# Two attention layers and two feed-forward layers on one core: the place of score products, the order of a second burst, and where constants are made

## The chip, the cores and the metric

The kernel runs on one core of a Trainium2 chip. The metric is the device time of one execution, in microseconds. TensorE (PE) multiplies matrices, VectorE (DVE) and ScalarE (ACT) read its results from PSUM, GpSimd (POOL) works from SBUF only, and SyncE (SP) issues the DMAs. PSUM has eight banks here: seven are handed out in rotation (`BANKS = 7`), one belongs to the weighted values.

## What is computed

The input has 4 batches of 2048 tokens with 256 features, in float32. Four sublayers follow each other, each on the layer-normalized input and each added to it:

```python
x = x + _L0_attn_ref(_layernorm(x), ...)   # one causal head, keys and values of 64
x = x + _L0_ffn_ref(_layernorm(x), ...)    # clipped to 8-bit floats, one matrix, a bias
x = x + _L1_attn_ref(_layernorm(x), ...)   # 16 causal heads of 16, rotary positions
x = x + _L1_ffn_ref(_layernorm(x), ...)    # mix with the token before; sigmoid(r) * (relu(k)**2 @ W_v)
```

## The kernel before

**Tiles.** The tokens are cut into 16 blocks of 512, four per batch (`order` lists them as b, qb). A block attends to itself and to the blocks before it in its batch. In the second attention the 16 heads form four groups of four (`HG = 4`); each of a group's heads sits in 32 partitions, so that a product of one head uses one of four row groups of the PE array, and the four heads' products can run beside each other.

**Steps.** The main loop goes over blocks, groups (index G) and tiles of 128 keys (`kt`); a block with index qb has 4, 8, 12 or 16 steps per group, 640 steps in all. In a step each head gets *scores* (`scores_of`): one bank, three products (L809), namely ones times the shift `sh` (the negated maximum of each query, in three bfloat16 parts), and the keys times the high and the low part of the queries. On the diagonal, that is in the last four steps of a group, fewer columns remain (512, 384, 256, 128) and two mask products (L817) follow. ScalarE then makes the exponential p (L824). The *weighted values* (`weighted`, L860) multiply p with the values in column groups of the array.

**Maxima.** Scores need the maximum of each query ahead of them. `maxima_of` makes them for the group that follows: one bank per head, two products (L779), on the diagonal two masks (L788), and a reduction on VectorE (L794). `all_maxima` gives each set its due place, mostly one set of four heads per step.

**The order in a step.** Instructions of PE, ACT, DVE and POOL are issued in the order in which the program writes them. A step writes, in this order: a *first burst* with scores of heads 0 and 1 and maxima of heads 2 and 3; the products that turn a finished group to tokens, if there is one; the weighted values of the step *before*; a *second burst* with maxima of heads 0 and 1 and scores of heads 2 and 3; further maxima if more than one set is due; the shift of the next group at a group's end (`shift_of`); and pulled work, products of other stages for this or other blocks that use the whole array.

```python
together([[S[0]], [S[1]], M[2], M[3]], {h: S[h] for h in (2, 3) if kt})
weighted(*last)
together([M[0], M[1], [S[2]], [S[3]]])
pull(lists, 0.0)
```

`together` writes a burst in rounds, one product per head and round, and passes over a head that has not begun while `room(h)` finds no bank. Its `spare` heads are those whose score may begin in a row that has ended.

**The planner.** `Clock` keeps a book of estimated times while the program is written: when each engine, row group and bank comes free. `room(h)` counts the banks that this book shows as free 50 ns after the last product. `pull` takes generators of other stages (A: first attention and first feed-forward of blocks ahead; Bq and Q: projections, keys and queries of the second attention; E: what follows it) when the book shows their inputs ready and the step's credit lasts; `pull_first` takes the earliest; `force` empties a list.

**The head.** Constants (identities, causal masks, zeroed pads, `ones`, `mask_k`, `mask_q`) are made on POOL ahead of all else, and six DMAs on SP copy the last two to the other row groups. A loop then brings the first block through `a_in` (layer norm, transposition, queries, keys, values; in two halves `hf` of 256 tokens), `a_mid` (first attention), `a_out`, `b_in`, `b_project` (rotation on POOL), `b_keys` and `b_queries`, with the second block's list A2 behind it. In `a_in` the second half waits at its start until the first half's projections are written. `prepare` (seven VectorE operations on weights) is written when its first weight is due in the book within 1 us of PE's time, or when nothing else can be taken.

Of the kernel before, what the change touches and what calls it, by code (L numbers as in the profile page):

```python
# [13 lines left out]
F16 = mybir.dt.float16  # L14
F32R = mybir.dt.float32r
BF16 = mybir.dt.bfloat16
# [3 lines left out]
ALU = mybir.AluOpType  # L20
AX = mybir.AxisListType

P = 128
# [3 lines left out]
TT = BLK // P  # L27
# [3 lines left out]
HG = 4  # L31
NG = NH // HG
SLOT = 32
LN_EPS = 1e-5
NEG = -1e30
# [155 lines left out]
def seq_kernel(  # L191
# [21 lines left out]
    nc = tc.nc  # L213
# [4 lines left out]
    const = ctx.enter_context(tc.tile_pool(name="const", bufs=1))  # L218
    clock = Clock(nc)
# [6 lines left out]

    ident = const.tile([P, P], F32, name="ident")
    make_identity(nc, ident)
    ident_b = const.tile([P, P], BF16, name="ident_b")
    make_identity(nc, ident_b)  # L230
    ident_h = const.tile([P, P], F16, name="ident_h")
    make_identity(nc, ident_h)

    mask_b = const.tile([P, P], BF16, name="mask_b")
    make_causal_mask(nc, mask_b, mask_val=NEG)

    maskT_b = const.tile([P, P], BF16, name="maskT_b")
    nc.gpsimd.memset(maskT_b, 0.0)
    nc.gpsimd.affine_select(
        out=maskT_b, in_=maskT_b, pattern=[[1, P]], compare_op=ALU.is_ge,  # L240
        fill=NEG, base=0, channel_multiplier=-1,
    )
    mhalf = const.tile([P, TT], F32, name="mhalf")
    nc.gpsimd.memset(mhalf, -0.5)

# [17 lines left out]
    order = [(b, qb) for b in range(B) for qb in range(NB)]  # L263
# [54 lines left out]

    pads = []
    for i in range(3):
        t = const.tile([P, TT, HG, SLOT], BF16, name=f"pad{i}")
        nc.gpsimd.memset(t, 0.0)
        pads.append(t)
    ones = const.tile([P, P], BF16, name="ones")
    nc.gpsimd.memset(ones, 0.0)
    for h in range(HG):
        nc.gpsimd.memset(ones[h * SLOT : h * SLOT + 3, :], 1.0)

# [1 line left out]

    mask_k = const.tile([P, 2, P], BF16, name="mask_k")
    mask_q = const.tile([P, 2, P], BF16, name="mask_q")
    for t, first, picks in (
        (mask_k, 0.0, ((ALU.not_equal, 2.0**-22, 0), (ALU.not_equal, 2.0**62, 1))),
        (mask_q, -(2.0**62), ((ALU.is_ge, 0.0, 0), (ALU.not_equal, -(2.0**-22), 0))),  # L340
    ):
        nc.gpsimd.memset(t[:SLOT], first)
        for keep, fill, base in picks:
            nc.gpsimd.affine_select(
                out=t[:SLOT], in_=t[:SLOT], pattern=[[P // 2, 2], [-1, P]],
                compare_op=keep, fill=fill, base=base, channel_multiplier=2,
            )
        for h in range(1, HG):
            nc.sync.dma_start(t[h * SLOT : (h + 1) * SLOT], t[:SLOT])

# [4 lines left out]
    live = [0]  # L355
# [21 lines left out]
    def done(n):  # L377
        live[0] -= n
# [83 lines left out]
    def a_in(b, qb, x, hf):  # L462

        tag = f"a0_{b}_{qb}"
        while hf and (b, qb, "a", 0) not in flags:
            yield None
        to = []
        yield from normal_T(x, to, hf, tag)
        xT = to[0]
        t2 = slice(2 * hf, 2 * hf + 2)  # L470
        nc.gpsimd.tensor_tensor(
            x[:, t2, :], x[:, t2, :], bo_bc[:, None, :].to_broadcast([P, 2, C]), ALU.add
        )
# [12 lines left out]
        nc.scalar.activation(th[:, cols], pq, AF.Identity, bias=bqk)  # L486
        nc.vector.scalar_tensor_tensor(
            tl[:, cols], pq, bqk, th[:, cols].bitcast(F32), ALU.add, ALU.subtract
        )
        if hf:  # L490

            for dst, src in (
                (qh[:D0], th[:D0]), (qh[D0:], th[:D0]), (kT[:D0], th[D0:]),
                (ql[:D0], tl[:D0]), (ql[D0:], tl[:D0]), (kT[D0:], tl[D0:]),
            ):
                nc.sync.dma_start(dst.bitcast(F32), src.bitcast(F32))
# [12 lines left out]
        flags.add((b, qb, "in", hf))  # L509
# [287 lines left out]
    def scores_of(b, qb, g, kt, sh, pTs, h):  # L797

        r = slice(h * SLOT, (h + 1) * SLOT)
        c0 = max(kt - qb * TT, 0) * P  # L800
        keys = kT1[b, kt // TT][r, g, (kt % TT) * P : (kt % TT + 1) * P]
        diag = kt >= qb * TT
        sc = bank(f"s_{b}_{qb}_{g}_{kt}_{h}")

        q = q1[b, qb, g // 2]
        todo = [(keys, z[r, g % 2, c0:]) for z in q]
        todo.insert(0 if kt else 2, (ones[r, :], sh[r, c0:]))
        for i, (lhsT, rhs) in enumerate(todo):
            nc.tensor.matmul(  # L809
                sc[:, c0:], lhsT, rhs, start=(i == 0), stop=(i == 2 and not diag)  # L810
            )
# [12 lines left out]
        nc.scalar.activation(pTs[h][:, c0:], sc[:, c0:], AF.Exp, scale=DK**-0.5)  # L824
        yield

    def room(h):

        clock.follow()
        now = max(clock.issue, clock.rows[h]) + 50  # L830
        return sum(b not in clock.held and t <= now for b, t in clock.banks.items())

    def together(rows, spare=()):

        rows = [[[part, False] for part in r] for r in rows]
        spare = dict(spare)
        wait = True
        while any(rows):  # L840
            moved = False
            for h, r in enumerate(rows):
                while r:
                    if wait and not r[0][1] and not room(h):
                        break
                    try:
                        next(r[0][0])
                        r[0][1] = moved = True
                        wait = True
                        break  # L850
                    except StopIteration:
                        r.pop(0)
                if not r and h in spare and any(rows) and room(h) > 3:
                    next(spare.pop(h))
            wait = moved

# [284 lines left out]
    a_next = 2  # L1141
    live[0] += 3
    prepared = False
    while Bq or Q or len(A2) > 2:
        credit = 1.0
        if not pull([Bq, Q, A], 0.0):
            credit = 0.1
            if not pull([A2], 0.0):
                ripe = not prepared and clock.when(wfs[0]) < clock.pe + 1000
                if ripe or not pull_first([Bq, Q, A, A2]):  # L1150
                    assert not prepared, (live, [(g.__name__, asked.get(id(g))) for l in (Bq, Q, A, A2) for g in l])
                    prepare()
                    done(3)
                    clock.follow()
                    prepared = True
        while narrow:
            narrow_values()
    A.extend(A2)
# [31 lines left out]
    for G, (i, b, qb, g) in enumerate(groups):  # L1190
# [5 lines left out]
        for kt in range(n):  # L1196
# [19 lines left out]
            if last is not None:  # L1216
# [4 lines left out]
                if last[2] != g:  # L1221
# [105 lines left out]
```

## Time and profile before

| | us |
|---|---|
| median of 3 runs | 2928.36 (2923.62, 2928.36, 2931.43) |
| the profiled execution | 2922.84 |
| its span, first to last instruction | 2921.0 |
| L809, three score products per head, busy | 672.6 + 494.3 + 481.0 |
| L779, two maxima products per head, busy | 686.1 + 559.3 |
| L860, weighted values, busy | 641.0 |
| L824, exponentials on ACT, busy; mean of one | 1214.2; 0.534 |
| L794, reductions on DVE, busy; mean of one | 1405.1; 0.603 |

The span is what lies between the first and the last instruction on the chip; the execution's own time is 1.8 us longer. Busy times of PE overlap, since up to four row groups work at once: the L809 and L779 rows can't be added up to the span, and a busy PE may have empty row groups. Steps of the main loop run from 115.3 us (first score product) to 2883.7 us (start of the last weighted group).

### The profile page before, as it was taken

The numbers are of one execution on the slowest core, as the hardware profiler recorded it, in microseconds if no ns is written. First come the engines' busy times: TensorE is split into PE (matmuls) and PEld (weight loads), VectorE is DVE, ScalarE is ACT, GpSimd is POOL, SyncE is SP. The second block draws the span as 40 slices with busy tenths as digits, with TensorE's granted clock in tenths as the row PEclk, the third lists the DMA queues.
The fourth block names the chain that finished last, engine by engine and source line by source line (L and its number), as shares of the span: only waits on it lengthen the run. The fifth ranks groups of instructions, "written<-read, shape, count | busy, mean of one in ns | idle before, by whom it ended". The sixth has DMA issues, their size and how long they took to land.

```text
span 2921.0 us, 68258 instructions
## 1 busy us (share of the span) xinstructions
PE 2804.3 (96%) x27616; PEld 1580.6 (54%) x27616; DVE 2012.6 (69%) x4279; ACT 1688.2 (58%) x3553; POOL 1011.8 (35%) x1534
## 2 busy tenths in 40 slices
PE   6899999999999999999999999999999999999997
PEld 3555555555456555555556555555545655555443
DVE  4567667787556786787746777778764677678761
ACT  2456555566665556656665555656566565665663
POOL 4534425242333514514215342523323342450001
PEclk8799999999999999999999999999999999999999
DMA  3000000000000000000000000000000000000000
GB/s 91 1 12 5 12 12 16 12 2 26 2 12 16 5 23 2 16 12 5 23 12 5 12 5 23 5 23 1 27 2 12 16 5 16 1 9 1 5 1 12
DMA packets 28781, 36.70 MB, mean 13 GB/s; under 512 B 3312, under 2 KB 22064, under 8 KB 28464
## 3 DMA queue, kind: packets, MB, share of 16 engines
q1 hardware_dynamic: 28464, 32.32, 3.9%
q8 instruction: 217, 3.56, 0.5%
q14 instruction: 100, 0.82, 0.1%
HBM read 11.24 MB, written 8.39 MB: 7 GB/s over the span
## 4 chain that ended last, share of the span: by engine, by line
PE 79%; DVE 11%; POOL 5%; issue 3%; ACT 1%; DMA 0%; SPq 0%; POOLq 0%; ACTq 0%; DVEq 0%
PE av L860 18%; PE s L809 16%; PE m L779 14%; DVE mx L794 7%; PE pq_a L421 3%; PE pv_a L421 2%; PE av_a L578 2%; PE m_a L524 2%; PE po_f L421 2%; PE pk_f L928 2%; PE pw_f L421 2%; PE pr_f L421 2%; PE m L788 1%; PE s_a L548 1%; PE pt_c L871 1%
## 5 line engine op out<-in xcount | busy, mean ns | idle before, releaser
L794 DVE TENSOR_REDUCE mx<-m 128x1 f32<-128x512 f32 (+3 forms) x2560 | 1405.1, 603 | 531.6 <-PE m L779 237.6
L824 ACT ACTIVATE p<-s 128x512 f32<-128x512 f32 (+3 forms) x2560 | 1214.2, 534 | 814.3 <-PE s L809 445.8
L779 PE MATMUL m<-kT_a,qh_a 32*128 32x512 f32 (+3 forms) x2560 | 686.1, 458 | 13.7 <-ACT p L824 4.0
L809 PE MATMUL s<-qh_a,kT_a 32*128 32x512 f32 (+3 forms) x2560 | 672.6, 508 | 0.5 <-ACT p L824 0.5
L860 PE MATMUL av<-p,v_a 128*32 128x512 f32 (+3 forms) x5120 | 641.0, 545 | 0.1
L779 PEld LDWEIGHTS m<-kT_a,qh_a 32*128 32x128 f32 x2560 | 296.0, 184 | 493.9 <-issue 161.1
L779 PE MATMUL m<-kT_a,ql_a 32*128 32x512 f32 (+3 forms) x2560 | 559.3, 368 | 0.0
L809 PE MATMUL s<-ql_a,kT_a 32*128 32x512 f32 (+3 forms) x2560 | 494.3, 365 | 0.0
L809 PE MATMUL s<-sh,ones 32*128 32x512 bf16 (+3 forms) x2560 | 481.0, 355 | 3.1 <-DVE mx L794 2.3
L779 PEld LDWEIGHTS m<-kT_a,ql_a 32*128 32x128 f32 x2560 | 297.0, 188 | 3.3 <-issue 1.0
L809 PEld LDWEIGHTS s<-qh_a,kT_a 32*128 32x128 f32 x2560 | 259.7, 189 | 35.3 <-issue 23.7
L809 PEld LDWEIGHTS s<-ql_a,kT_a 32*128 32x128 f32 x2560 | 257.3, 187 | 2.8 <-issue 0.2
L809 PEld LDWEIGHTS <-ones 32*128 32x128 bf16 x2560 | 128.7, 91 | 171.4 <-issue 150.5
L860 PEld LDWEIGHTS av<-p,v_a 128*32 128x32 f32 x5120 | 112.4, 108 | 161.8 <-issue 118.7
L443 POOL CAST pad<-nm 128x16 bf16<-128x16 f32 x64 | 17.0, 266 | 380.9 <-DVE nm L989 352.3
L590 POOL TENSOR_TENSOR sum_a<-sum_a,p_a 128x512 f32<-128x512 f32 (+1 forms) x128 | 146.3, 1143 | 5.0
L788 PE MATMUL m<-mask_k,mask_q 32*128 32x64 bf16 x2048 | 147.0, 196 | 0.0
L817 PE MATMUL s<-mask_q,mask_k 32*128 32x64 bf16 (+1 forms) x2048 | 140.4, 207 | 0.0
L590 POOL TENSOR_TENSOR cx_a<-cx_a,avs_a 128x512 f32<-128x512 f32 (+1 forms) x64 | 73.1, 1143 | 155.1 <-ACT avs_a L588 155.1
L421 PE MATMUL pq_a<-wqkv,xT_a 128*128 128x512 f32 x256 | 122.8, 602 | 1.6 <-DVE mx L794 1.3
L950 POOL TENSOR_TENSOR x<-x,sg_f 128x512 f32<-128x512 f32 x32 | 41.4, 1294 | 177.3 <-DVE sg_f L949 177.1
L935 POOL TENSOR_TENSOR ka_f<-ka_f 128x512 f32<-128x512 f32 x32 | 33.2, 1038 | 186.1 <-ACT ka_f L934 186.1
(164 smaller groups left out, 4015.6 us busy)
## 6 DMA issues: line engine op xcount, KB each, us to landing
x<-in_x SPq DMA_DIRECT2D x16, 512.0 KB, 4.0
out_y<-x SPq DMA_DIRECT2D x32, 256.0 KB, 2.1
qh_a<-th_a SPq DMA_DIRECT2D x32, 128.0 KB, 2.3
ql_a<-tl_a SPq DMA_DIRECT2D x32, 128.0 KB, 2.3
kT_a<-th_a SPq DMA_DIRECT2D x16, 128.0 KB, 2.3
kT_a<-tl_a SPq DMA_DIRECT2D x16, 128.0 KB, 2.3
wqkv<-in_wqkv1T SPq DMA_DIRECT2D x1, 768.0 KB, 7.3
wc<-in_wfT SPq DMA_DIRECT2D x1, 256.0 KB, 5.7
```

Of the source, the lines that this page charges most:

```text
L421: nc.tensor.matmul(dst, lhsT[:, k, t * P : (t + 1) * P], w[:, k, :], start=(k == 0), stop=(k == CK - 1),)
L524: nc.tensor.matmul(sc[:, :w], q[:, t * P : (t + 1) * P], kT0[kb][:, :w], start=(q is qh), stop=(kb < qb and q is ql),)
L578: nc.tensor.matmul(av[z * SLOT : (z + 1) * SLOT, c0:], v0[kt // TT][:, kt % TT + j, d * SLOT : (d + 1) * SLOT], pTs[j][:, c0:], start=True ...
L590: nc.gpsimd.tensor_tensor(to[:, c0:], to[:, c0:], add[:, c0:], ALU.add)
L779: nc.tensor.matmul(sc[:, :w], q1[b, qb, g // 2][i][r, g % 2, t * P : (t + 1) * P], kT1[b, kb][r, g, :w], start=(i == 0), stop=(kb < qb and ...
L788: nc.tensor.matmul(sc[:, w - P + lo : w - P // 2 + lo], mask_q[r, v, :], mask_k[r, v, lo : lo + P // 2], start=False, stop=(v == 1),)
L794: nc.vector.reduce_max(mx[:, t, h, kb : kb + 1], sc[:, :w], axis=AX.X)
L809: nc.tensor.matmul(sc[:, c0:], lhsT, rhs, start=(i == 0), stop=(i == 2 and not diag))
L817: nc.tensor.matmul(sc[:, c0 : c0 + hi], mask_k[r, v, :], mask_q[r, v, :hi], start=False, stop=(v == 1),)
L824: nc.scalar.activation(pTs[h][:, c0:], sc[:, c0:], AF.Exp, scale=DK**-0.5)
L860: nc.tensor.matmul(av[h * SLOT : (h + 1) * SLOT, c0:], v1[b, kt // TT][:, kt % TT, at : at + SLOT], pTs[h][:, c0:], start=(kt == 0), stop= ...
L928: nc.tensor.matmul(pk[:, d * HALF : (d + 1) * HALF], wk[:, k, d * P : (d + 1) * P], xk[:, k, :], start=(k == 0), stop=(k == CK - 1),)
```

## The change

Three parts, in one diff.

1. *First bursts.* A spare score (head 2 or 3) begins if `room(h)` is over 0 instead of over 3. A head that begins so is noted in `early`, and its products then stand in the order keys times high queries, ones times shift, keys times low queries, so that what is written in the first burst is a product with the keys. In the second burst the remaining two follow.
2. *Second bursts.* Heads are gone through in the order 2, 3, 0, 1: scores of 2 and 3 ahead of maxima of 0 and 1.
3. *The head of the run.* All constants but the float32 identity, `mhalf` and `one` move into `constants()`, written once the first block's first half has begun its projections, with the six DMAs. In the first block the second half's layer norm and transposition no longer wait for the first half's projections; its own projections still do. `prepare` is written once the second half's values are projected. The line with 1000000000.0 is never true, so the second block's list is asked as before when nothing else is ready.

```diff
-    ident_b = const.tile([P, P], BF16, name="ident_b")
-    make_identity(nc, ident_b)
...
-        for h in range(1, HG):
-            nc.sync.dma_start(t[h * SLOT : (h + 1) * SLOT], t[:SLOT])
+
+    def constants():
+
+        make_identity(nc, ident_b)
+
+        make_causal_mask(nc, mask_b, mask_val=NEG)
+
+        nc.gpsimd.memset(maskT_b, 0.0)
...
+        for t in reversed(pads):
+            nc.gpsimd.memset(t, 0.0)
...
+        make_identity(nc, ident_h)
...
+            for h in range(1, HG):
+                nc.sync.dma_start(t[h * SLOT : (h + 1) * SLOT], t[:SLOT])
...
-        while hf and (b, qb, "a", 0) not in flags:
+        while hf and (b, qb) != order[0] and (b, qb, "a", 0) not in flags:
             yield None
         to = []
         yield from normal_T(x, to, hf, tag)
         xT = to[0]
+        while hf and (b, qb, "a", 0) not in flags:
+            yield None
...
-        todo.insert(0 if kt else 2, (ones[r, :], sh[r, c0:]))
+        todo.insert((1 if h in early else 0) if kt else 2, (ones[r, :], sh[r, c0:]))
...
+    early = set()
+
...
-    def together(rows, spare=()):
+    def together(rows, spare=(), order=range(HG)):
...
-            for h, r in enumerate(rows):
+            for h in order:
+                r = rows[h]
...
-                if not r and h in spare and any(rows) and room(h) > 3:
+                if not r and h in spare and any(rows) and room(h) > 0:
+                    early.add(h)
                     next(spare.pop(h))
...
+    made = False
     while Bq or Q or len(A2) > 2:
+        if not made and (*order[0], "a", 0) in flags:
+            constants()
+            clock.follow()
+            made = True
+        if not prepared and (*order[0], "in", 1) in flags:
+            prepare()
+            done(3)
+            clock.follow()
+            prepared = True
...
-            if not pull([A2], 0.0):
-                ripe = not prepared and clock.when(wfs[0]) < clock.pe + 1000
-                if ripe or not pull_first([Bq, Q, A, A2]):
...
+            ahead = [clock.free[e] for e in ("act", "dve", "pool")]
+            if (ready and max(ahead) > ready + 1000000000.0) or not pull([A2], 0.0):
+                some = pull_first([Bq, Q, A, A2])
...
+            early.clear()
             together([[S[0]], [S[1]], M[2], M[3]], {h: S[h] for h in (2, 3) if kt})
...
-            together([M[0], M[1], [S[2]], [S[3]]])
+            together([M[0], M[1], [S[2]], [S[3]]], order=(2, 3, 0, 1))
```

More of the change, by code (lines that the diff above doesn't have):

```diff
@@ L228, in seq_kernel @@
     make_identity(nc, ident)
-    ident_b = const.tile([P, P], BF16, name="ident_b")
-    make_identity(nc, ident_b)
[L231 to L242, printed above, removed]
     mhalf = const.tile([P, TT], F32, name="mhalf")
@@ L313, in prepare @@
         nc.vector.tensor_scalar_mul(wv_flat, wv_flat, 0.5)
[L321 to L325, printed above, removed]
+    ident_b = const.tile([P, P], BF16, name="ident_b")
+    ident_h = const.tile([P, P], F16, name="ident_h")
+    mask_b = const.tile([P, P], BF16, name="mask_b")
+    maskT_b = const.tile([P, P], BF16, name="maskT_b")
+    pads = [const.tile([P, TT, HG, SLOT], BF16, name=f"pad{i}") for i in range(3)]
@@ L326, in seq_kernel @@
     ones = const.tile([P, P], BF16, name="ones")
-    nc.gpsimd.memset(ones, 0.0)
-    for h in range(HG):
-        nc.gpsimd.memset(ones[h * SLOT : h * SLOT + 3, :], 1.0)
     mask_k = const.tile([P, 2, P], BF16, name="mask_k")
     mask_q = const.tile([P, 2, P], BF16, name="mask_q")
[L338 to L347, printed above, removed]
-        for h in range(1, HG):
-            nc.sync.dma_start(t[h * SLOT : (h + 1) * SLOT], t[:SLOT])
+    def constants():
+        make_identity(nc, ident_b)
+        make_causal_mask(nc, mask_b, mask_val=NEG)
+        nc.gpsimd.memset(maskT_b, 0.0)
+        nc.gpsimd.affine_select(
+            out=maskT_b, in_=maskT_b, pattern=[[1, P]], compare_op=ALU.is_ge,
+            fill=NEG, base=0, channel_multiplier=-1,
+        )
+        for t in reversed(pads):
+            nc.gpsimd.memset(t, 0.0)
+        nc.gpsimd.memset(ones, 0.0)
+        for h in range(HG):
+            nc.gpsimd.memset(ones[h * SLOT : h * SLOT + 3, :], 1.0)
+        make_identity(nc, ident_h)
+        for t, first, picks in (
+            (mask_k, 0.0, ((ALU.not_equal, 2.0**-22, 0), (ALU.not_equal, 2.0**62, 1))),
+            (mask_q, -(2.0**62), ((ALU.is_ge, 0.0, 0), (ALU.not_equal, -(2.0**-22), 0))),
+        ):
+            nc.gpsimd.memset(t[:SLOT], first)
+            for keep, fill, base in picks:
+                nc.gpsimd.affine_select(
+                    out=t[:SLOT], in_=t[:SLOT], pattern=[[P // 2, 2], [-1, P]],
+                    compare_op=keep, fill=fill, base=base, channel_multiplier=2,
+                )
+            for h in range(1, HG):
+                nc.sync.dma_start(t[h * SLOT : (h + 1) * SLOT], t[:SLOT])
@@ L1147, in seq_kernel @@
             credit = 0.1
-            if not pull([A2], 0.0):
-                ripe = not prepared and clock.when(wfs[0]) < clock.pe + 1000
-                if ripe or not pull_first([Bq, Q, A, A2]):
[L1151 to L1155, printed above, removed]
+            ready = [start_of(gens, gen) for gens in (Bq, Q, A) for gen in list(gens)]
+            ready = min([t for t in ready if t is not None] or [0.0])
+            ahead = [clock.free[e] for e in ("act", "dve", "pool")]
+            if (ready and max(ahead) > ready + 1000000000.0) or not pull([A2], 0.0):
+                some = pull_first([Bq, Q, A, A2])
+                if not some:
+                    assert some, (live, [(g.__name__, asked.get(id(g))) for l in (Bq, Q, A, A2) for g in l])
         while narrow:
```

## The prediction

> **What bounds the kernel now.** I read the page first, then busy time by stage, then the order of time inside a few steps of the main loop, and last the head of the run.
>
> ```profile
> span 2921.0 us, 68258 instructions
> PE 2804.3 (96%) x27616; PEld 1580.6 (54%) x27616; DVE 2012.6 (69%) x4279; ACT 1688.2 (58%) x3553; POOL 1011.8 (35%) x1534
> PE 79%; DVE 11%; POOL 5%; issue 3%; ACT 1%; DMA 0%; SPq 0%; POOLq 0%; ACTq 0%; DVEq 0%
> ```
>
> TensorE is busy for 96% of the span and 79% of the chain that ended last lies on it. By stage:
>
> ```profile
> 0.00:33.00 33.00, 13.54 (x54) 11.02 (x54) 14.10 (x37) 4.46 (x7) 15.44 (x42) 0.86 0.56 177
> 33.00:115.00 82.00, 62.28 (x348) 41.24 (x348) 37.15 (x105) 23.85 (x48) 52.18 (x74) 0.81 0.05 10
> 115.00:2866.00 2751.00, 2688.42 (x26970) 1505.65 (x26968) 1950.16 (x4111) 1643.73 (x3463) 934.86 (x1405) 0.99 0.04 11
> ```
>
> (Columns: length, then busy time of PE, weight loads, DVE, ACT, POOL, granted clock, DMA share and rate.) From 115 us to 2866 us PE is busy for 2688 of 2751 us at a clock of 0.99: only less PE time per step helps there. The head is another regime: 76 of 115 us busy. So the question is what a step costs on PE, and a "busy" product may use only two of the four row groups. Two steps in order of time:
>
> ```profile
> 1505.22 0.39 PE L809 MATMUL s<-sh,ones 32*128 32x512 bf16 x2
> 1505.26 0.58 PE L809 MATMUL s<-qh_a,kT_a 32*128 32x512 f32 x2
> 1505.68 0.40 PE L809 MATMUL s<-ql_a,kT_a 32*128 32x512 f32 x2
> 1506.01 0.65 PE L415 MATMUL pt_a<-ident,xn_a 128*128 128x128 f32 x4
> 1506.60 0.39 PE L809 MATMUL s<-sh,ones 32*128 32x512 bf16 x2
> 1506.64 0.58 PE L809 MATMUL s<-qh_a,kT_a 32*128 32x512 f32 x2
> 1507.06 0.40 PE L809 MATMUL s<-ql_a,kT_a 32*128 32x512 f32 x2
> 1507.39 1.07 PE L860 MATMUL av<-p,v_a 128*32 128x512 f32 x8
> 1508.39 0.39 PE L809 MATMUL s<-sh,ones 32*128 32x512 bf16 x2
> ```
>
> At 1505.22 a second burst: heads 2 and 3, three products each, 0.79 us to the next work. At 1506.01 a pulled transpose on the whole array. At 1506.60 the first burst of the next step: heads 0 and 1, three products, while rows 2 and 3 stand empty. Then the weighted values, and at 1508.39 heads 2 and 3 once more. In the burst at 1506.60 there is room for the first product of heads 2 and 3. One product of 512 columns takes 0.23 us: (1505.68 - 1505.22) / 2, from the start of the first to the start of the third.
>
> **First-burst products, the main part.** In the old code the spare rows start a score only with more than three banks free. Counting score products (L809) up to each weighted group shows that this happened 19 times in 640 steps. Now one free bank does, in the 576 steps with kt above 0. Per step one product moves from the second burst to rows that are idle in the first (maxima have two products, scores three). Nothing is added: the same 7680 score products.
>
> Where does it pay? Bursts that follow each other with nothing between run rows independently: rows 0 and 1 do two maxima and three score products, rows 2 and 3 three and two, five each, and moving one from a burst to the burst before changes no sum. It pays where whole-array work is pulled between second burst and next first burst, since there the array drains and the time is 3 + 3 products against 2 + 3. Such work stands behind 424 of the 576 steps; 257 of them have full width (512 columns). The other 167 are on the diagonal (384, 256, 128 columns): there maxima of two long products already outlast three short score products, so the moved product lengthens the first burst about as much as it shortens the second. Summing row lengths over those steps gives a gain of 0 to 3 us; I take 0.
>
> Both rows must be granted a bank, for with one row still at three products the second burst is as long as before. I paired each PSUM tile's first product with the instruction that empties it, and counted banks outside such pairs 50 ns after the second head's third product began. Of the 257 full, pulled steps 197 had one free or more and 120 two or more. As a test of this count: more than three were free in 13 steps, against 19 that the old rule granted. So 120 x 0.23 = 28 us as it stands; 257 x 0.23 = 59 us if every grant came; about 1 us if the kernel's own book of bank times has one bank fewer free than the trace. Counted 0.4 us later, at that product's end, 169 steps have two free (39 us). I take 140 steps, nearer to the first count: 32 us.
>
> A check of "idle rows cost nothing": 166 second bursts with maxima beside the scores (four rows) took 0.88 us from first start to last end, the one at 1508.39 with two rows 0.85 us. Two more rows cost 0.02 us over three products, so nothing is charged. The Trainium skill, page "TensorE: Matmul & The Clock Gate", section "Measured speedup vs the span model", has a rule against it: four row tiles give 3.07 times, not four times. By that a filled slot would cost 0.3 of a product and the 32 us would become an estimated 22. The two bursts above differ by far less, and they decide.
>
> **Order of the second burst.** Scores of heads 2 and 3 go ahead of maxima of heads 0 and 1. The maxima's bank wait no longer stands before the scores; behind the scores stand only the maxima, then their reductions on VectorE, needed a group later. In the trace the second burst starts 0.52 us after the last weighted product in the median of 303 full-width cases (mean 0.525), which is the mode change, so few banks are missing there and the order alone gains or loses little: bounds plus and minus 3 us, value 0.
>
> **The exponentials' chain.** Weighted products wait for p of heads 2 and 3 in few steps: 51 groups are over 0.1 us longer than their width asks for, 37 us in all, 48 of them without pulled work behind the burst. There the earlier scores start ACT earlier by one product: 32 of them had a free bank; each gains one product or what its wait lasts, whichever is less: 6 us together. Bounds 0 and 10.
>
> **Constants, first half, prepare.** 22 POOL instructions (1.31 to 8.42 us without mhalf and one) and six DMAs on SP leave the head.
>
> ```profile
> 8.42 0.22 POOL L395 TENSOR_SCALAR v_a<-mv_a 128x2 f32<-128x2 f32 x1
> 8.72 0.72 POOL L397 TENSOR_TENSOR y_a<-v_a,mhalf 128x2 f32<-128x2 f32 x1
> 14.34 1.85 SPq L349 DMA_DIRECT2D mask_k<-mask_k  x3
> 16.29 1.80 SPq L349 DMA_DIRECT2D mask_q<-mask_q  x3
> 20.23 0.71 POOL L397 TENSOR_TENSOR y_a<-v_a,mhalf 128x2 f32<-128x2 f32 x1
> 29.09 0.60 SPq L496 DMA_DIRECT2D kT_a<-tl_a  x1
> 32.74 0.46 PE L524 MATMUL m_a<-kT_a,qh_a 128*128 128x128 f32 x1
> ```
>
> The first y (the scale of the layer norm, made on POOL) starts at 8.72 because the constants stand ahead; its statistics are done at 6.08, so it comes 2.3 us earlier. The second half's y of the first block stood at 20.23, because the half was only begun behind the first projections, with the 4.3 us of the seven VectorE operations of the old early preparation between (13.36 to 18.18). Now its statistics follow the first half's at once: y near 8. So the queries and keys, whose last copy was issued at 29.09 and was landed for the first product at 32.74, could be ready some 15 us earlier but for what is late next. The constants, 6.9 us on POOL, now begin behind the first x + bo (about 9.5) and end near 16.4; the mask DMAs (1.85 + 1.80 us of SP) wait for them, to about 20; the six copies of q and k (3.7 us) may stand behind those on SP, to 24, and landing takes 2.3 us by the page: 26 or so against 32. Six us at that point. Preparation now runs behind the second half's projections, while PE waits for the copies; if that cover is gone, 4.3 us of VectorE stand before the first maxima's reductions. Masks, ones and pads are first read at 33 us and later, which hides POOL's part; but y and x + bo of the second block are queued behind the constants on POOL, up to 6.9 us late, and from 63 to 80 us POOL is full with that block's sums, for which the first block's rotation (80 to 99) waits. So not all six arrive at 115 us, where the steps begin. Value 5 us, bounds -7 (the constants' length given back by the second block) and +12.
>
> **Sum.** 32 + 0 + 0 + 6 + 5 = 43 us. The profiled execution took 2922.84 us (span 2921.0 and 1.8 around it), so 2880; it was the fastest of four, 5.5 us below the median of 2928.36, and I forecast a median: 2885 us. Its own range: main part 1 to 59, taken as 15 to 50 for the likely cases, others as above: 2865 to 2910.
>
> **Rivals.**
> (a) *Banks take the place.* Early scores hold two of seven banks through the weighted products (1.0 us), and transposes to tokens, narrow values and the maxima of the second burst look for one. For it: no bank was free in 183 of 576 decisions, and maxima of the first burst already stand still for a bank of VectorE in 80 cases, 28.5 us, 0.36 each. If the second burst's maxima wait as long behind 250 early steps, 90 us are lost against 43 won: 2975; it decides from 120 such waits on. Against it: a bank is only taken if one is free, two would be taken at the burst's start anyway, and no stall stands there now. The Trainium skill, "Trainium Kernel Development and Optimization", Best Practices, warns that tiling speeds up TensorE but not the emptying of PSUM; no row here gives that a price beyond the waits counted. Chance 0.15.
> (b) *The grants do not come, or the room is used up*: the book of bank times refuses as before, or pulled work that is now early waits for its inputs instead (VectorE is 71% busy in the main stage, 1950 of 2751). Then 0 to 10 us are left, from the head and the exponentials: 2923. Chance 0.15.
> (c) *All grants come*: 59 + 10 + 10 = 79 us: 2849. For it: less waiting frees banks earlier. Against: ACT and VectorE free banks at their own pace while the next decision comes earlier too. Chance 0.15.
> Forecast: 0.55.
>
> **How the numbers follow.** 2885 is the forecast's. Of (a) nearly all lies above 2937, of (c) half below 2849; the range 2848 to 2936 leaves 0.07 below and 0.13 above. What a measurement can tell from no change is about 0.3%, 9 us: 2919.6 to 2937.1. Faster: 0.53 of the forecast, all of (c), 0.04 of (b), together 0.72. Same: 0.02 of the forecast, 0.07 of (b), 0.01 of (a): 0.10. Slower: 0.14 of (a), 0.04 of (b): 0.18.
>
> **What would show it.** Right: many second bursts with four instead of six score products; in pulled steps 0.56 us instead of 0.79 from burst to next work; score products with qh standing ahead of ones in first bursts; PE's busy time in the main stage down by about what the span loses; the first full-array maxima (L524 now) near 26 us. Wrong: bursts of six as before (b); weight loads of maxima idle behind VectorE in second bursts (a); no shorter burst although the grants came, which would mean that the four rows do not run side by side; the first steps beginning later than 115 us, which would put the head's sign wrong.

## The result, and the profile after

The changed kernel takes 2967.75 us in the median of 4 runs (2966.5 to 2976.93), the kernel before 2928.52 beside it: ratio 1.0142, interval 1.0118 to 1.0167. It is slower by 39 us; 2885 was forecast.

The page of the changed kernel: span, engines' busy time, chain by engine.

```profile
span 2966.7 us, 68223 instructions
PE 2843.0 (96%) x27616; PEld 1613.6 (54%) x27616; DVE 2027.5 (68%) x4279; ACT 1690.7 (57%) x3553; POOL 1013.6 (34%) x1534
PE 79%; DVE 10%; POOL 5%; issue 3%; ACT 2%; DMA 0%; POOLq 0%; ACTq 0%; DVEq 0%
```

The same 27616 products make PE busy 39 us longer; no other engine gained as much. By stage (columns as before; the steps of the main loop begin at 129 us now, 115 before):

```profile
33.00:129.00 96.00, 70.52 (x356) 45.91 (x356) 39.01 (x105) 24.68 (x49) 52.67 (x73) 0.73 0.04 9
129.00:2929.00 2800.00, 2736.27 (x27122) 1540.26 (x27120) 1963.03 (x4111) 1655.37 (x3486) 935.07 (x1404) 0.98 0.04 11
```

So the head is 14 us longer, and the steps are longer as well: from the first weighted group to the last 2794.4 us against 2762.2. I gave the time from each product's start to the next one's to the kind of the earlier one. Bursts went from 1226.1 to 1256.7 us, weighted products from 587.3 to 582.8, pulled work from 948.8 to 954.9. The loss stands in the bursts, where the gain was forecast. Not all of it is what the products of a burst cost: the clock granted to TensorE fell to 0.5 for 121.3 us of the changed kernel's steps and for 66.2 us of the steps before. What that is worth comes at the end of the experiments.

The grants came: counted as before, 252 steps started both spare scores and 283 one. A first burst of the kernel before, with pulled work ahead of it, in order of time:

```profile
434.90 0.39 PE L809 MATMUL s<-sh,ones 32*128 32x512 bf16 x2
434.90 0.50 PE L779 MATMUL m<-kT_a,qh_a 32*128 32x512 f32 x2
434.94 0.58 PE L809 MATMUL s<-qh_a,kT_a 32*128 32x512 f32 x2
435.24 0.40 PE L779 MATMUL m<-kT_a,ql_a 32*128 32x512 f32 x2
435.36 0.40 PE L809 MATMUL s<-ql_a,kT_a 32*128 32x512 f32 x2
435.69 0.64 PE L860 MATMUL av<-p,v_a 128*32 128x512 f32 x4
```

The same kind of burst of the changed kernel, with both spare scores, and a second burst relieved of them:

```profile
1044.07 0.39 PE L811 MATMUL s<-sh,ones 32*128 32x512 bf16 x2
1044.08 0.50 PE L781 MATMUL m<-kT_a,qh_a 32*128 32x512 f32 x2
1044.11 0.58 PE L811 MATMUL s<-qh_a,kT_a 32*128 32x512 f32 x2
1044.41 0.40 PE L781 MATMUL m<-kT_a,ql_a 32*128 32x512 f32 x2
1044.53 0.39 PE L811 MATMUL s<-ql_a,kT_a 32*128 32x512 f32 x2
1044.64 0.40 PE L811 MATMUL s<-qh_a,kT_a 32*128 32x512 f32 x2
1044.97 0.64 PE L866 MATMUL av<-p,v_a 128*32 128x512 f32 x4
...
735.40 0.39 PE L811 MATMUL s<-sh,ones 32*128 32x512 bf16 x2
735.41 0.49 PE L781 MATMUL m<-kT_a,qh_a 32*128 32x512 f32 x2
735.44 0.58 PE L811 MATMUL s<-ql_a,kT_a 32*128 32x512 f32 x2
735.74 0.40 PE L781 MATMUL m<-kT_a,ql_a 32*128 32x512 f32 x2
736.07 0.40 PE L453 MATMUL pt_sh_a<-ident_b,pad 128*128 128x128 bf16 x4
```

Read the starts within one row group. A row that opens with ones (bfloat16) starts its third product 0.46 us after its first (434.90 to 435.36). A row that opens with keys or queries (float32) starts its *second* 0.33 us after the first (1044.08 to 1044.41), and its third at 0.56 (1044.64). So the maxima's row with a third product ends 0.1 us after the score rows beside it: the first burst lasts 0.90 us to the weighted group, instead of 0.79. And the second burst, 0.67 us, goes by the maxima's rows, which open with float32, so it saves 0.13 us and not 0.23.

### The profile page after: what moved, and what is told of

Same layout as the page of the kernel before. It is cut to its first block, busy times and chain, and to the rows that moved or that the text cites. A ratio compares the mean times of both kernels' runs of the same rounds, so it can differ in the third digit from the quotient of the medians.

```text
span 2966.7 us, 68223 instructions
## 1 busy us (share of the span) xinstructions
PE 2843.0 (96%) x27616; PEld 1613.6 (54%) x27616; DVE 2027.5 (68%) x4279; ACT 1690.7 (57%) x3553; POOL 1013.6 (34%) x1534
## 4 chain that ended last, share of the span: by engine, by line
PE 79%; DVE 10%; POOL 5%; issue 3%; ACT 2%; DMA 0%; POOLq 0%; ACTq 0%; DVEq 0%
PE s L811 20%; PE av L866 18%; PE m L781 10%; DVE mx L796 6%; PE pq_a L421 3%; PE pv_a L421 2%; PE av_a L580 2%; PE pk_f L934 2%; PE po_f L421 2%; PE m_a L526 2%; PE pr_f L421 2%; PE pw_f L421 2%; ACT p L826 1%; PE pt_c L877 1%; PE pq_a L486 1%
## 5 line engine op out<-in xcount | busy, mean ns | idle before, releaser
L811 PE MATMUL s<-qh_a,kT_a 32*128 32x512 f32 (+3 forms) x2560 | 733.1, 481 | 4.9 <-ACT p L826 3.4
L781 PE MATMUL m<-kT_a,qh_a 32*128 32x512 f32 (+3 forms) x2560 | 704.9, 462 | 15.7 <-ACT p L826 10.2
L811 PE MATMUL s<-ql_a,kT_a 32*128 32x512 f32 (+3 forms) x2560 | 629.1, 413 | 0.0
L781 PE MATMUL m<-kT_a,ql_a 32*128 32x512 f32 (+3 forms) x2560 | 574.8, 370 | 0.0
L811 PE MATMUL s<-sh,ones 32*128 32x512 bf16 (+3 forms) x2560 | 469.2, 357 | 6.1 <-DVE mx L796 4.9
L781 PEld LDWEIGHTS m<-kT_a,qh_a 32*128 32x128 f32 x2560 | 307.1, 185 | 77.0 <-ACT p L826 36.1
L811 PEld LDWEIGHTS s<-qh_a,kT_a 32*128 32x128 f32 x2560 | 303.5, 188 | 66.4 <-ACT p L826 21.6
L811 PEld LDWEIGHTS s<-ql_a,kT_a 32*128 32x128 f32 x2560 | 305.0, 190 | 2.3
L819 PE MATMUL s<-mask_q,mask_k 32*128 32x128 bf16 (+1 forms) x2048 | 157.1, 208 | 0.0
L532 DVE TENSOR_REDUCE mx_a<-m_a 128x1 f32<-128x512 f32 (+3 forms) x160 | 87.5, 602 | 18.4 <-PE m_a L526 16.2
```

Source lines behind the costliest of these rows:

```text
L532: nc.vector.reduce_max(mx[:, t, kb : kb + 1], sc[:, :w], axis=AX.X)
L781: nc.tensor.matmul(sc[:, :w], q1[b, qb, g // 2][i][r, g % 2, t * P : (t + 1) * P], kT1[b, kb][r, g, :w], start=(i == 0), stop=(kb < qb and ...
L811: nc.tensor.matmul(sc[:, c0:], lhsT, rhs, start=(i == 0), stop=(i == 2 and not diag))
L819: nc.tensor.matmul(sc[:, c0 : c0 + hi], mask_k[r, v, :], mask_q[r, v, :hi], start=False, stop=(v == 1),)
```

## The experiments

All times are medians, with the ratio to the kernel before on the same chip and its 95% interval. "Deal" means which pulled work stands in which step. A "live" planner decides anew while the program is written.

**The three parts alone, and double grants.** Four kernels: the kernel before with part 3, part 1 or part 2, and the changed kernel with this condition:

```diff
-                if not r and h in spare and any(rows) and room(h) > 0:
-                    early.add(h)
-                    next(spare.pop(h))
+                if h == 3 and len(spare) == 2 and not rows[2] and not r and any(rows) and room(h) > 1:
+                    for z in (2, 3):
+                        early.add(z)
+                        next(spare.pop(z))
```

> The kernel before with part 3 alone (constants, first half, prepare). Theory: the changed kernel's first score product stands at 129.1 us against 115.3 before and its steps lose 32 us in the bursts; these are two separate costs, so this kernel is 12 to 16 us slower than before (2941 to 2945 us) and its bursts sum up as before (1226 us, within 8). Rival, the planner: the later start deals pulled work out differently, and that is what lengthens the bursts; then this kernel is 35 to 50 us slower (2965 to 2975).

Measured: 2930.36 us, 1.0005 (0.9995 to 1.0014). A miss: the first score product stands at 130.9 us, 15.6 later, but the steps take 10.6 us less (bursts 1223.8 us, as forecast). That the second block's work is further on when they begin would explain it, but was not tried by itself. The head is worth nothing either way.

> The kernel before with part 1 alone (spare scores from one free bank). Theory, the leading product: after a mode change a row group whose first product has float32 weights gets its second 0.34 us later, one led by ones 0.23 us later; so a first burst with the moved product lasts 0.90 us instead of 0.79, a second burst relieved of it in both rows 0.67 instead of 0.80, and one relieved in one row 0.78. Two grants then gain nothing and one grant loses 0.1 us: 250 to 300 single grants make this kernel 20 to 35 us slower (2948 to 2963). Rival, planner or head: within 8 us of before (2920 to 2937).

Measured: 2975.99 us, 1.0162 (1.0138 to 1.0185): above the range, on the theory's side. Bursts 1271.0 us, 45 more than before.

> The kernel before with part 2 alone (scores of heads 2 and 3 written ahead of the maxima in second bursts). Theory: rows are independent and no bank is missing at the start of second bursts, so nothing changes but what the planner deals differently: within 8 us of before (2920 to 2937). Rival: the later maxima hold their banks into the next first burst, whose maxima and scores then wait: 15 to 35 us slower (2943 to 2963).

Measured: 2967.51 us, 1.0130 (1.0104 to 1.0155). Slower by 38 us: the theory fell, and this stood at the rival's size, until the next experiment took the two things in it apart.

> The changed kernel, but spare scores begin only when both rows have a bank, so no single grants. Theory, the leading product: single grants (283 steps) are the loss in the bursts, 0.1 us each; without them 20 to 35 us come back: 2933 to 2948 us, with the head's 13 us still lost. Rival, banks held early: about as many steps still hold two banks through the weighted products, so the time stays at 2955 or more.

Measured: 2962.63 us, 1.0121 (1.0104 to 1.0138), 5 us below the changed kernel. A miss, though 233 double grants and no single ones were made: with part 2 in it this kernel has the changed kernel's deal (in no group does the count of pulled products differ), and what that goes with is in the table below.

**The deal held fixed.** Part 2 moves nothing but maxima, and yet other blocks' work was pulled elsewhere. So I wrote down every decision of the planner, to pull or not to pull, and read it back in kernels with other bursts:

```diff
-                    if t is None or t > clock.pe + SLACK:
+                    if t is None:
                         continue
+                    late = t > clock.pe + SLACK
...
+                    if not plan.of(0 if late else 1):
+                        continue
```

> The kernel before with part 2 alone, and with the planner's decisions of the kernel before written down and read back (which stage's work is pulled in which step, 4363 decisions): every instruction outside the bursts stands where it stood before. Part 2 with a live planner was 38 us slower. Theory, the deal: the order itself costs nothing, its book entries made the planner pull other work; within 10 us of before (2919 to 2939). Rival, late maxima: their banks and reductions come later whatever the deal; 25 us or more slower (2954 or more).

Measured: 2936.97 us, 1.0031 (1.0019 to 1.0042). With the deal held, the order costs 6 us by the medians and 9 by the ratio; some 30 of its 38 came with the deal.

> The kernel before with part 1 alone and the deal of before read back. Part 1 with a live planner was 47 us slower, 45 of them in the bursts. Theory, the leading product: the loss stands in the bursts themselves, so 20 to 40 us of it stay (2949 to 2969), and first bursts with one moved product are longer by 0.1 us in the median. Rival, the deal: within 10 us of before.

Measured: 2982.36 us, 1.0179 (1.0149 to 1.0210), above the range. Since the deal is the same, each burst can be set against its own before (means, pulled work on one side):

| burst | grants | cases | longer by, us |
|---|---|---|---|
| first, full width | both | 136 | 0.114 |
| first, full width | one | 91 | 0.122 |
| first, diagonal | both | 125 | 0.135 |
| first, diagonal | one | 17 | 0.215 |
| second, full width | both | 97 | -0.170 |
| second, full width | one | 120 | -0.005 |
| second, diagonal | both | 99 | -0.065 |
| second, diagonal | one | 39 | -0.029 |

All first bursts together lose 47.7 us and all second bursts gain 13.8; bursts in one piece between two weighted groups lose 10.8, those with pulled work on both sides 2.5. The sum, 47.2, is the loss between the two profiled executions. Of it 36.5 us stand in the 1055 bursts that both traces show at the full clock: first bursts 44.2 longer, second 20.5 shorter. A single grant costs time in the first burst and gets nothing in the second; the diagonal, which I had set to nothing, loses most per grant.

> The kernel before with parts 1 and 2 and the deal of before read back. Theory, the leading product: as with part 1 alone, 15 to 40 us slower (2944 to 2969). Rival, the deal: within 10 us of before. If parts 1 and 2 were meant to go together, this is the faster of the two: below 2920.

Measured: 2962.38 us, 1.0115 (1.0090 to 1.0139). In the theory's range; the order takes 20 us off part 1's loss, without making a gain of it. The range is met partly for another reason: the bursts lose 33 us in all, but only 12 of them in bursts at the full clock in both traces.

> The changed kernel's head and the changed kernel's deal read back (4320 decisions), but with the bursts of before. If the deal alone makes the changed kernel slow: 2950 to 2970. If its bursts alone do: 2922 to 2938. If half each: 2940 to 2950.

Measured: 2975.68 us, 1.0155 (1.0131 to 1.0179): the changed kernel's head and deal lose 45 us with the old bursts. The third block of a batch (qb = 2) shows where; from its first weighted group to the next block's, in us:

| kernel | bursts | deal | batch 1 | batch 2 | of it at a clock of 0.5 |
|---|---|---|---|---|---|
| before | old | old | 212.6 | 214.4 | 0, 3.4 |
| e1_head | old | old from batch 1 on | 214.3 | 214.2 | 3.4, 3.4 |
| r_b_order | part 2 | old | 212.4 | 214.0 | 0, 3.4 |
| r_b_both | parts 1, 2 | old | 217.5 | 216.3 | 6.8, 4.5 |
| e3_order | part 2 | new | 226.0 | 227.0 | 17.1, 18.9 |
| r_a_none | old | new | 228.5 | 228.4 | 20.5, 20.5 |
| e4_both | double grants, part 2 | new | 225.2 | 222.0 | 13.5, 6.8 |
| changed kernel | parts 1, 2 | new | 226.3 | 229.0 | 11.2, 17.7 |

Every kernel with the new deal loses 8 to 16 us in each such block, whatever its bursts. In the second block it pulls less (batch 2: 268 products against 293), in the third more (460 against 435). Blocks 2 and 3 of batch 2 together, with the same products and the same order in the bursts, take 358.8 us in r_b_order and 368.8 in e3_order; bursts are 5.4 longer there, weighted groups 1.7, transposes of the feed-forward input 1.7, the rest in small amounts. That every kind of work is longer fits the last column: the two blocks stand at a clock of 0.5 for 6.8 us in r_b_order and for 23.9 in e3_order.

**The leading product by itself.** The spare rule is the old one and no bank is held longer; only the order inside every score changes, in the old deal:

```diff
-        todo.insert(0 if kt else 2, (ones[r, :], sh[r, c0:]))
+        todo.insert(1 if kt else 2, (ones[r, :], sh[r, c0:]))
```

> The kernel before, its deal read back, no spare scores added; only the order inside a score is changed: keys times high queries first, ones second, for all kt above 0. Nothing is held longer. Theory, the leading product: rows of three products that open with float32 weights last 0.90 us instead of 0.79, so full-width first and second bursts with pulled work on one side (some 430 of each, 575 of the 865 at full width) get 0.11 us longer, together 60 to 95 us: 2990 to 3025 us. Rival, banks held early (what made part 1 slow is the holding): within 10 us of before.

Measured, in two runs: 2994.16 us, 1.0219 (1.0193 to 1.0244). A first burst of it:

```profile
344.97 0.50 PE L830 MATMUL s<-qh_a,kT_a 32*128 32x512 f32 x2
344.98 0.50 PE L800 MATMUL m<-kT_a,qh_a 32*128 32x512 f32 x2
...
345.32 0.39 PE L830 MATMUL s<-sh,ones 32*128 32x512 bf16 x2
...
345.36 0.57 PE L830 MATMUL s<-ql_a,kT_a 32*128 32x512 f32 x2
345.86 0.64 PE L881 MATMUL av<-p,v_a 128*32 128x512 f32 x4
```

0.89 us from first product to weighted group, where the kernel before has 0.79 with the same three products. (Here the third product starts 0.39 us after the first, for the ones stand right before it, but it lasts 0.57 instead of 0.40.) The bursts' sum grew by 63 us, 59 of them in bursts at the full clock in both traces; first and second bursts at full width by 0.10 in the median each. So what a burst costs goes by which product leads, not by what is held.

**Only the grants that can pay.** Part 1 in the old deal, for both rows at once and at full width:

> Part 1 in the deal of before, granted only to both rows at once and only at full width (136 grants instead of 541 on one row or two). Theory, the leading product: a first burst gets 0.11 us longer and a second burst with pulled work behind it 0.14 to 0.17 shorter, the diagonal's and the single grants' loss is gone: between 8 us faster and 8 us slower than before (2921 to 2939). Rival, banks held early: 136 of 541 grants keep a quarter of the 51 us, 2940 or more.

Measured: 2925.25 us, 0.9978 (0.9964 to 0.9993). As forecast: first bursts 11.9 us more in 111 cases, second 13.7 less in 81. These two nearly cancel; most of the 7 us gained stands elsewhere.

**Ones ahead of the maxima.** If a row of three is cheap when ones lead it, the spare score's ones product belongs in front of the maxima. Rows 2 and 3 then run ones, maxima, maxima, and the score's two others follow in the second burst:

```diff
+    def led(score, maxima):
+
+        next(score)
+        yield
+        yield from maxima
...
+            if ms and 0 < kt <= qb * TT and room(2) >= 4:
+                opened = [S[2], S[3]]
+                together([[S[0]], [S[1]], [led(S[2], M[2][0])], [led(S[3], M[3][0])]])
```

> The kernel before in its deal, with a new form: where four banks or more are free as a full-width first burst begins (160 steps), rows 2 and 3 open with the ones product of their own score, and the maxima follow it. Theory, the leading product: such a row lasts 0.79 us like the score rows beside it, so the first burst costs nothing, and a second burst of two products per row lasts 0.66 instead of 0.80: some 105 of the 160 have pulled work behind, 14 us faster (2910 to 2922). If the row's length goes by the number of products alone, also faster by 14 to 24. Rival, banks: maxima wait for theirs behind the opened score; 2935 or more.

Measured: 2941.40 us, 1.0047 (1.0032 to 1.0062). A miss: second bursts gave 14.2 us in 102 cases, as forecast, but first bursts lost 28.9 in 133. One of them:

```profile
1009.64 0.40 PE L830 MATMUL s<-sh,ones 32*128 32x512 bf16 x4
1009.68 0.58 PE L830 MATMUL s<-qh_a,kT_a 32*128 32x512 f32 x2
1009.68 0.81 PE L800 MATMUL m<-kT_a,qh_a 32*128 32x512 f32 x2
1010.00 0.18 PEld L800 LDWEIGHTS m<-kT_a,qh_a 32*128 32x128 f32 x1 [0.16 <-ACT v_a L718]
1010.10 0.40 PE L830 MATMUL s<-ql_a,kT_a 32*128 32x512 f32 x2
1010.11 0.62 PE L800 MATMUL m<-kT_a,ql_a 32*128 32x512 f32 x2
1010.66 0.64 PE L887 MATMUL av<-p,v_a 128*32 128x512 f32 x4
```

The two maxima no longer start together (0.81 us for a pair that takes 0.58): the second one's weights are loaded (PEld) at 1010.00, once ScalarE has copied v_a out of its bank. The burst lasts 1.02 us. By the count of free banks as such a burst began in the kernel before, the burst grew by 0.45 us in the mean with four (34 cases), 0.22 with five (40) and 0.004 with six (53). So this is the bank wait that rival (a) spoke of: such a burst opens four scores and two sets of maxima, and needs a bank for each of the six.

> The same with a live planner. Theory: the bursts gain as with the deal read back, and the planner's book of row times, changed a little, may keep the deal of before (about 2915) or fall into the other one that the order of part 2 brought (2945 to 2960).

Measured: 2956.18 us, 1.0087 (1.0072 to 1.0102): another deal (by the trace, 135 pulled products stand in another group than before) adds 15 us.

> As l_b_4, but only where six banks are free as the first burst begins, one for each head that opens in it (58 steps instead of 160). Theory, leading product and banks as separate costs: no first burst grows (median within 0.01 us), second bursts with pulled work behind shrink by 0.13 us in some 40 steps: 5 us faster (2922 to 2928 beside a before of 2930). Rival, a held bank costs time later on: first bursts free but other bursts longer, 2932 or more.

Measured: 2926.33 us, 0.9982 (0.9971 to 0.9993). As forecast, first bursts grew by 0.004 us in the mean (47 cases), second shrank by 0.110 in 37. Its first burst:

```profile
611.03 0.39 PE L830 MATMUL s<-sh,ones 32*128 32x512 bf16 x4
611.07 0.58 PE L830 MATMUL s<-qh_a,kT_a 32*128 32x512 f32 x2
611.08 0.58 PE L800 MATMUL m<-kT_a,qh_a 32*128 32x512 f32 x2
611.49 0.39 PE L830 MATMUL s<-ql_a,kT_a 32*128 32x512 f32 x2
611.49 0.40 PE L800 MATMUL m<-kT_a,ql_a 32*128 32x512 f32 x2
611.83 1.06 PE L887 MATMUL av<-p,v_a 128*32 128x512 f32 x8
```

Four rows of three products, all done in 0.80 us.

> l_b_6 and r_b_full2 together in the deal of before: ones ahead of the maxima where six banks are free, else spare scores in both rows at full width (148 steps on the whole). Theory: the first form costs nothing and the second 0.11 us in its first burst, both win 0.13 to 0.17 where pulled work follows: 8 to 14 us faster (2916 to 2922 beside a before of 2930). Rival: no better than r_b_full2, 6 us faster.

Measured: 2923.18 us, 0.9979 (0.9966 to 0.9992), 6.5 us faster than before; no better than r_b_full2 by its interval, so the rival's size.

> The same with a live planner, whose deal differs from that of before in 19 of 64 groups, but not in the middle blocks of a batch, where parts 2 and 1 together lost 14 us each. Theory: 2912 to 2926. Rival: any other deal than the old one is slower, 2940 or more.

Measured: 2924.76 us, 0.9985 (0.9975 to 0.9996). The idea can gain, then, but 0.1 to 0.2%, with few grants at the right places.

**The clock beside all this.** The trace also has the clock granted to TensorE: the full one, or half of it in stretches of 3.4 us or a few times that. The third block of batch 2 in r_a_none, and a part of it (columns as before; the clock stands third from the end):

```profile
1802.10:2030.50 228.40, 221.95 (x2089) 122.00 (x2088) 163.26 (x332) 131.64 (x272) 76.52 (x107) 0.96 0.05 13
1914.80:1928.40 13.60, 12.87 (x95) 6.62 (x93) 6.94 (x17) 6.73 (x14) 3.75 (x7) 0.50 0.13 39
```

What such a stretch costs can be read where kernels differ in it alone. In the kernels with the old deal 149 bursts, weighted groups and stretches of pulled work stand wholly at 0.5 in one and, with the same products, wholly at the full clock in another: 212.2 us against 125.2, so 0.41 us are lost in each us at 0.5. One burst of ten products lasts 0.89 us at 197.76 in the kernel before and 1.60 at 203.22 in l_b_6. From the first weighted group to the last, beside the kernel before:

| kernel | steps longer by, us | at 0.5 for longer by, us | estimated cost of that, us |
|---|---|---|---|
| changed kernel | 32.2 | 55.1 | 23 |
| e3_order | 44.0 | 81.1 | 33 |
| r_a_none | 40.3 | 75.0 | 31 |
| r_b_order | 12.2 | 38.3 | 16 |
| r_b_both | 43.8 | 96.4 | 40 |
| r_b_part1 | 45.4 | 48.0 | 20 |
| f_b_second | 63.8 | 10.7 | 4 |

The last column is an estimate, 0.41 times the one before it, from one profiled execution of each. The lower clock is in the other runs too: over a whole execution 0.966 to 0.972 in those of the changed kernel, 0.973 to 0.980 in those of the kernel before. So the deal's loss, and that of parts 1 and 2 together, is mostly time at the lower clock; the loss of f_b_second is not. What opens such a stretch was not tried. Idle time of TensorE stands ahead of many, as the 1.38 us before 1912.21 in r_a_none, in which it waited for VectorE's maxima; but of 11 idle gaps of over 1 us in the steps of the kernel before only 6 are followed by one within 5 us.

## Why the prediction was wrong

**The step that failed** is the sentence "two more rows cost 0.02 us over three products, so nothing is charged" for the moved product. I compared bursts of four rows with bursts of two (0.88 and 0.85 us, which is 0.03), but in both the longest row was led by ones. The moved product makes a row of three led by float32, and that row costs 0.11 us more. The trace of before had it: the maxima's second product at 435.24 stands 0.34 us behind the first, the score's third at 435.36 only 0.46 behind its first. Second bursts gave 0.135 us in the median for both grants instead of 0.23, since the same maxima became their longest row. Where 32 us of gain were forecast, part 1 in the old deal made a loss of 47 in the bursts, 36.5 of them at the full clock.

**A second step** is a term that the sum does not have. I read a clock of 0.99 in the main stage and concluded that "only less PE time per step helps there", as if it would stay. In the changed kernel's steps 55 us more stand at a clock of 0.5, an estimated 23 of the 32 us that they are longer.

**Both rows must be granted**: right (-0.170 us against -0.005). But I let a single grant cost nothing; it costs 0.12 at full width, and the changed kernel made 283 of them. **The diagonal at zero**: wrong, first bursts there lost 16.9 us with both grants and second gained 6.5.

**The order at 0, bounds 3**: in the bursts about right, for with the deal held those at the full clock in both traces are 2 us shorter in sum; the 6 to 9 us of r_b_order stand beside 38 us more at a clock of 0.5. On the whole it was wrong. I had not considered that the planner reads the book that the order writes, and so deals other work; with that 38 us.

**The exponentials' chain, 6 us**: the sign was right, weighted groups went from 587.3 to 582.8 us, though 27.2 instead of 12.4 us of them stand at a clock of 0.5. No run takes this term by itself, so its size stays open.

**The head, 5 us, bounds -7 and 12**: its net in e1_head is 1 us lost or nothing, in the range. By the prediction's own sign its direction was wrong, for the steps begin later than at 115 us, and what makes up for it came from the steps, not from the head. The working was right up to the copies and wrong behind them: the last copy of keys is issued at 25.67 instead of 29.09, yet the first maxima start at 36.27 instead of 32.74.

```profile
25.67 0.59 SPq L498 DMA_DIRECT2D kT_a<-tl_a  x1
...
29.67 0.71 POOL L397 TENSOR_TENSOR y_a<-v_a,mhalf 128x2 f32<-128x2 f32 x1
...
32.84 2.08 PE L486 MATMUL pq_a<-xT_a,wqk 128*128 128x256 f32 x4 [0.73 <-ACT xT_a L416]
...
36.27 0.45 PE L526 MATMUL m_a<-kT_a,qh_a 128*128 128x128 f32 x1
```

The second block's second half, its y at 29.67 and its projections at 32.84, is now written ahead of the first block's maxima, and PE keeps that order. I had priced queues on POOL and SP and forgotten PE's own.

**The range, 2865 to 2910**: with 15 to 50 us for the main part and the other bounds as stated, the gains add up to 5 to 75 us, that is 2853 to 2923; the narrower range does not follow from them.

**Rivals.** (a) had the sign, and 2975 comes near the 2967.75 measured, but that is luck: its bank waits are real (l_b_4), yet f_b_second loses 62 us with no bank held longer, and no run shows such waits as what slowed this kernel. (b) and (c) did not occur. None of the three had the clock.

**What the 39 us are made of.** Head: nothing. Deal and bursts do not add up: with the old bursts the new deal costs 45 us, with the old deal the new bursts cost 31, both together 39. Either way most of the loss stands beside more time at a clock of 0.5: an estimated 31 of 40 us of the steps in r_a_none, 40 of 44 in r_b_both, 23 of 32 in the changed kernel. Of the 31 us that the changed kernel's bursts lose, an estimated 10 are the clock's (50.6 us of them at 0.5, 25.4 before); the rest fits the leading product. Another part of the overlap: with the new deal and the old bursts, first bursts with pulled work ahead are already at 0.907 us in the mean (0.873 before), and part 1 adds less to those. Of the 14 to 16 us that a third block loses in r_a_none, 17 to 21 us more at a clock of 0.5 make an estimated 7 to 8, and 25 pulled products more than before stand in it; why the clock falls there stays open.

## What to carry to other kernels

Before a product is moved into an idle row, read the starts within that row, not the burst's length: the row that gets it may become the longest, and what leads it decides by how much. A slot that is filled only for some rows of a group pays its cost and wins nothing. Where a planner orders work by its own book, hold its decisions fixed to measure a local change; otherwise one measures its other choice. And before a difference between two kernels is shared out among their parts, compare the granted clock in each: with every decision held fixed, it still differed here.

## What the runs showed of the hardware

Behind work of another shape (whole-array products, or weighted ones in column groups), a burst whose rows of three products are led by bfloat16 ones lasts 0.79 to 0.80 us, and 0.89 to 0.90 if a float32 product leads one of them; the weight loads of the two last 0.091 and about 0.185 us. Reordering three products of every score cost 62 us of 2932 on that account. Whether the weights' type or the moving operand's makes it was not tried; ones and shift are both bfloat16.

At a granted clock of 0.5 the same products took 212.2 us where they took 125.2 at the full clock (149 cases in the kernels with the old deal). Such stretches make up 66 us of the 2762 us of steps before, and 121 of 2794 in the changed kernel.
